# Where a preparation step is done: layer 2's weights and the image norms of samples 1 to 3, in a four-layer network on one NeuronCore

## The chip, the core and the metric

The kernel runs on one core of one Trainium2 chip. A core has five engines that run side by side, each working through its own instructions in order: TensorE (PE in the profile; its weight loads are PEld), VectorE (DVE), ScalarE (ACT), GpSimd (POOL) and SyncE (SP), which here issues nearly all transfers between the core's memory and DRAM. An instruction that depends on another engine or on a transfer waits for a semaphore, and all that stands behind it on its engine waits with it. The metric is the device time of one execution in microseconds (us); lower is better.

## The reference, cut to what matters

The input x is float32, (4, 56, 56, 128): four samples, 56 x 56 positions, 128 channels. Four layers follow, each a residual around a group norm:

```python
x = x + L0(gn(x))    # 7x7 window attention, then attention over all 3136 positions, then an MLP
x = x + L1(gn(x))    # for each node: sum over 56 partners of relu(a_i + b_j), then a linear layer
x = x + L2(gn(x))    # Fourier layers: keys, queries, values, attention over 128 channels, projection, ...
x = x + L3(gn(x))    # a convolution over one axis with its row and column sums
```

Layer 2 treats each of the 128 channels of a sample as a 56 x 56 image. What the change touches is its beginning:

```python
xa = x.reshape(B * T, 1, H, W)                     # T = 128 images in each of B = 4 samples
xa_n = _inorm(xa, norm_g[0], norm_b[0])            # (x - mean) * rsqrt(var + eps) over an image
k = _fno_layer(xa_n, wK, wKs, bKs, (H // 2, W // 2))   # rfft2, times weights per frequency, irfft2
q = _fno_layer(xa_n, wQ, wQs, bQs, (H // 2, W // 2))
v = _fno_layer(xa_n, wV, wVs, bVs, (H, W))
scores = jnp.einsum('bhtd,bhsd->bhts', qs, ks) / np.sqrt(ks.shape[-1])
```

The kernel works with the images' spectra. Scores come from spectra and from products of the key and query weights; values and projection are merged into one set of weights for each frequency. Both sets depend on the weights alone, not on x.

## The kernel before, in words

**Layers 0 and 1** run one sample after another (`first_layers`). Each sample has four stages: the 7x7 tiles (`fast_windows`, eight groups in a software pipeline whose order on PE, ACT and DVE is written out by hand), attention over all positions (lines 606 to 684), the MLP (lines 856 to 940) and the edge layer (lines 982 to 1050), which leaves the sample in the tile `x1`. One SP transfer then saves `x1` to DRAM (`x2d[b]`, line 2484), and another loads the next sample (`xw`, line 2477).

**Image norms.** `normed_images` is a Python generator: it issues a norm in small steps, each `yield` ending one. Its steps are 56 `bn_stats` over the rows of the images (line 1243, two to a step), one `bn_aggr` (1247), two small PE products with `k.g4` that average over groups of four channels (1250, 1259), about twenty short DVE operations on 128 x 56 or 128 x 1, two square roots on ACT (1274, 1301), two PE products over the 128 partitions' sums (1283, 1292), and four passes over the image that subtract the mean and scale (line 193 by way of `apply_norm`), after which SP stores the normed sample to `xad[b]` (1299). It keeps an inverse deviation for each image in `st.norm`. Before the change the norms of samples 0, 1 and 2 are dealt out between the stages of `fast_windows` of samples 1, 2 and 3 (`steps = beside(bank)`, one step after each pipeline stage).

**Spectra.** After the last edge layer, `spectra` transforms the four samples. `first_transform` of a sample makes four `s_pr` tiles (PE, 56 matmuls each in the profile, line 1322), scales each on DVE with the image's inverse deviation into `s_z` (1324) and copies it on ACT (1326). `sample_spectra` of a sample then issues thirteen steps: three `s_ps` (PE 1338, ACT copies 1341), two `s_pr2` (PE 1350, ACT 1354) and eight `s_px` (PE 1360, evacuated by DVE and ACT in turn, line 232 or 230). The four pieces of the next sample's `first_transform` are issued at steps 2, 5, 7 and 9, and the norm of sample 3, the only one left, at three of its steps after each step. PE, ACT and DVE keep the order in which all this is written. Samples 0 to 2 come from `xad` into two tiles `s_x2` (line 2516, two transfers of 784 KB each); sample 3 is still in `x1`.

**Layer 2's weights.** `all_score_weights` loads `qk4`, `qk` and `qkr` and combines them on GpSimd into `g` and `g4`; `value_weights` loads `V`, `Vrev` and `P`, combines them on GpSimd and stores the result to DRAM (`dd`). Both are issued just ahead of `spectra`, in the pool `g_wk`. `attention_weights`, which follows the spectra, is the first to read `g`.

**Queues around the change.** SP's transfers go out in program order. Where the program is not ordered by hand (SP, and GpSimd here), a scheduler sets the order. Behind the branch that joins the samples' loop, SP's order before is: the four loads of `s_x2` for samples 0 and 1, then `qk4` and `qk`, the store of `x1` to `x2d[3]`, eight small weights, `qkr`, `V`, `Vrev`, `P`, and the two loads for sample 2.

## Time and profile before

| | us |
|---|---|
| median of 6 runs | 3877.62 |
| lowest and highest of them | 3871.62, 3890.88 |
| the profiled execution, device time | 3868.63 |
| the profiled execution, span of its instructions | 3866.6 |
| 7x7 tiles of sample 0, first `w_xg` to first `f_s` | 98.86 |
| the same of samples 1, 2, 3 | 111.68, 111.77, 111.78 |
| spectra, first `s_pr` to first `q_u` on DVE | 2884.43 to 2971.58 |

Over the whole span PE is busy 91%, DVE 75%, ACT 54% and GpSimd 31%. The shares are averages over stages with different limits, so the stage that an edit lies in has to be looked at by itself. PEclk is the clock that TensorE was granted, as a share of full speed. A line of the timeline gives the start, the duration, the engine, the source line, the operation, the tile written and the tiles read, the shape, and how many equal instructions were merged; in brackets stands the idle time ahead of it and what ended that.

### The profile page before, as it was taken

How to read it: one execution, taken by the hardware profiler on the slowest of the kernel's cores; microseconds unless marked ns; L12 is line 12 of the kernel's file. 1: busy time of each engine (PE TensorE's matmuls, PEld its weight loads, DVE VectorE, ACT ScalarE, POOL GpSimd, SP SyncE). 2: the span in 40 equal slices, each digit the busy share in tenths (PEclk: the TensorE clock that was granted, in tenths of full speed). 3: DMA queues.
4: the chain of work that ended last, by engine and by line, in shares of the span. 5: the costliest groups of instructions: out<-in, count | busy, mean ns of one | idle time of the engine just before them, and what ended most of it. 6: DMA issues, size and time to landing. Idle time of an engine off the chain costs nothing. (4 is left out here: it accounts for less than half of the span.)

```text
span 3866.6 us, 79430 instructions
## 1 busy us (share of the span) xinstructions
PE 3537.0 (91%) x35416; PEld 1584.9 (41%) x35416; DVE 2896.0 (75%) x2703; ACT 2077.9 (54%) x2080; POOL 1210.9 (31%) x667
## 2 busy tenths in 40 slices
PE   6899999989998998999989989999998979989988
PEld 4322234543223455323245532223456433336564
DVE  6588877858887786788869758887776767765654
ACT  4577765548776554677745457776542012214332
POOL 0000016600000570000028300000655769975556
PEclk8999999999999999999999999999998999999888
DMA  2000000000000000000000000000011058841101
GB/s 96 1 1 1 1 1 19 19 17 1 1 1 1 18 3 34 1 1 1 1 17 3 19 18 1 1 1 34 2 42 51 1 119 171 171 107 59 52 8 50
DMA packets 73496, 111.12 MB, mean 29 GB/s; under 512 B 62140, under 2 KB 63932, under 8 KB 67900
## 3 DMA queue, kind: packets, MB, share of 16 engines
q1 hardware_dynamic: 14460, 93.13, 8.1%
q10 hardware_dynamic: 58688, 12.85, 2.0%
q8 instruction: 279, 4.57, 0.5%
q14 instruction: 69, 0.57, 0.1%
HBM read 79.46 MB, written 26.51 MB: 27 GB/s over the span
## 5 line engine op out<-in xcount | busy, mean ns | idle before, releaser
L663 ACT ACTIVATE f_ring<-f_s 128x1792 f32<-128x1792 f32 (+3 forms) x796 | 1097.3, 1429 | 226.6 <-PE f_s L661 224.8
L606 DVE TENSOR_TENSOR f_acc<-f_acc,f_ring 128x1792 f32<-128x1792 f32 x560 | 1133.9, 2025 | 64.3 <-ACT f_ring L663 7.5
L661 PE MATMUL f_s<-f_qT,f_kT 32*128 32x448 f32 x5376 | 738.4, 571 | 47.9 <-ACT f_ring L663 29.5
L877 POOL TENSOR_TENSOR m_sq<-m_y 128x392 f32<-128x392 f32 x16 | 14.5, 919 | 1973.8 <-ACT m_y L876 1973.7
L612 PE MATMUL f_po<-f_ring,f_va 128*32 128x448 f32 x5376 | 589.7, 546 | 0.0
L1029 DVE TENSOR_TENSOR e_td<-e_pa,e_c 128x1792 f32<-128x1792 f32 x252 | 491.2, 2012 | 14.4 <-ACT e_a L994 14.4
L1031 POOL TENSOR_TENSOR e_tp<-e_a,e_c 128x1792 f32<-128x1792 f32 x140 | 451.8, 3258 | 145.2 <-PE e_acc L1036 104.4
L661 PEld LDWEIGHTS f_s<-f_qT,f_kT 32*128 32x128 f32 x5376 | 268.3, 183 | 524.6 <-ACT f_ring L663 379.1
L1036 PE MATMUL e_acc<-e_td,t_shared 32*32 32x448 f32 x8064 | 324.0, 546 | 22.0 <-DVE e_td L1029 11.2
L1033 ACT ACTIVATE e_tp<-e_tp 128x1792 f32<-128x1792 f32 x140 | 235.1, 1697 | 176.4 <-POOL e_tp L1031 176.4
L1645 DVE TENSOR_TENSOR u_ud<-u_px,u_d 112x1792 f32<-112x1792 f32 x144 | 240.1, 1707 | 94.8 <-PE u_po L1650 85.7
L612 PEld LDWEIGHTS f_po<-f_ring,f_va 128*32 128x32 f32 x5376 | 133.0, 109 | 396.5 <-issue 395.5
L1036 PE MATMUL e_acc<-e_tp,t_shared 32*32 32x448 f32 x4480 | 222.4, 547 | 3.2 <-ACT e_tp L1033 2.5
L1650 PE MATMUL u_po<-u_ud,AT 112*64 112x448 f32 x960 | 200.7, 548 | 23.3 <-DVE u_ud L1645 23.3
L1647 POOL TENSOR_TENSOR u_up<-xh,u_d 112x1792 f32<-112x1792 f32 x64 | 193.8, 3056 | 24.0 <-PE u_po L1650 12.4
L1036 PEld LDWEIGHTS e_acc<-e_td,t_shared 32*32 32x32 f32 x8064 | 134.3, 103 | 146.3 <-DVE e_td L1029 55.9
L629 DVE RECIPROCAL f_den<-f_den 128x448 f32<-128x448 f32 x28 | 82.7, 2953 | 77.3 <-ACT f_den L628 77.3
L1650 PE MATMUL u_po<-u_up,AT 112*64 112x448 f32 x576 | 125.2, 541 | 0.8 <-POOL u_up L1647 0.8
L1650 PEld LDWEIGHTS u_po<-u_ud,AT 112*64 112x64 f32 x960 | 64.9, 137 | 147.6 <-issue 86.7
L606 DVE TENSOR_TENSOR f_acc<-f_ring 128x1792 f32<-128x1792 f32 x28 | 56.7, 2024 | 86.7 <-ACT f_ring L663 57.8
L1512 POOL TENSOR_TENSOR q_u<-iS,q_g 128x1792 f32<-128x1792 f32 x32 | 102.7, 3236 | 56.7 <-PE s_px L1360 32.5
L1036 PEld LDWEIGHTS e_acc<-e_tp,t_shared 32*32 32x32 f32 x4480 | 95.2, 103 | 55.4 <-ACT e_tp L1033 19.4
(485 smaller groups left out, 4785.0 us busy)
## 6 DMA issues: line engine op xcount, KB each, us to landing
u_d<-dd SPq DMA_DIRECT2D x48, 784.0 KB
xw<-in_x SPq DMA_DIRECT2D x4, 1568.0 KB
x2d<-x SPq DMA_DIRECT2D x4, 1568.0 KB
xad<-x SPq DMA_DIRECT2D x4, 1568.0 KB
x_xs<-xad ACTq DMA_DIRECT2D x32, 196.0 KB
xm<-x_ev ACTq DMA_DIRECT2D x64, 98.0 KB
o_a<-xm SPq DMA_DIRECT2D x8, 784.0 KB
o_x<-x2d SPq DMA_DIRECT2D x4, 1568.0 KB
```

The costliest lines, as they stand in the source:

```text
L606: nc.vector.tensor_add(acc, slots(j, 0) if c == 1 else acc, slots(j, c))
L612: nc.tensor.matmul(po[heads[h], :NB], va[o, c, heads[h]], p, start=(c == 0), stop=(c == 24))
L661: nc.tensor.matmul(ss[:, i, :NB], kT[heads[h], c * P:(c + 1) * P], qT[heads[h], blk(j)], start=True, stop=True)
L663: nc.scalar.activation(ring[:, slot:slot + m, :], ss[:, :m, :NB], AF.Exp, scale=scale)
L1029: nc.vector.tensor_tensor(t, am, cm, ALU.max)
L1031: nc.gpsimd.tensor_sub(t, bc(a.rearrange("p (l n) -> p l n", l=8), 1, 4), cm)
L1033: nc.scalar.activation(tf, tf, AF.Relu)
L1036: nc.tensor.matmul(acc[quarters[q], r, :NB], k.ident[o, o], t[o, q].rearrange("p l n -> p (l n)"), start=(g == 0), stop=(g == len(EDGE_TUR ...
L1512: nc.gpsimd.tensor_mul(u, bc(st.iS[:, bp, c, :HH], 1, HEADS), bc(g[:, n, c, :], 2, HH))
L1645: nc.vector.tensor_mul(u, bc(px[:, :, :NB], 2, m), dm)
L1647: nc.gpsimd.tensor_mul(u, bc(x, 2, m), dm)
L1650: nc.tensor.matmul(po[64 * b2:64 * b2 + 64, :NB], st.AT[:, 8 * i + h0 + q, 2 * bp + b2, :], u[:, b2, q, :], start=(left == 16), stop=(left ...
```

## The change

Three things are edited.

1. Layer 2's weights are made in sample 0's pass: `norms(0, ...)` calls `layer2_weights()` and returns an empty iterator. The score weights go to DRAM as one tile `gd` of 17 columns and are loaded back into `g` ahead of the spectra. `value_weights` no longer copies into a third tile; it stores from `d` and from `V`.
2. Of the norms, only sample 0's stays beside 7x7 tiles (those of sample 1). The tiles of samples 2 and 3 carry none. Samples 1 and 2 are read for the spectra from `x2d`, not yet normed.
3. In `spectra` the order of samples becomes 0, 3, 1, 2. The norms of 3, 1 and 2 are dealt out one after another, three steps after each piece of sample 0's first transform and four after each step of `sample_spectra`. The next sample's first transform is issued at steps 8 to 11; ahead of its first piece, the steps of that sample's norm that are left are issued.

```diff
@@ spectra
-        norm = normed_images(k, w, st, B - 1, wk, lambda: tiny.tile([P, 512], F32, name="s_pt"), st.x1, xad[B - 1])
+        order = [0, B - 1, *range(1, B - 1)]
+        def of(b):
+            return st.x1 if b == B - 1 else images(b)
+        def steps(n):
+            for norm in norms[:1]:
+                for _ in range(n):
+                    if next(norm, norm) is norm:
+                        norms.pop(0)
+                        break
+        norms = [normed_images(k, w, st, b, wk, lambda: tiny.tile([P, 512], F32, name="s_pt"), of(b), xad[b])
+                 for b in order[1:]]
         zs = {}
-        first = [first_transform(k, st, b, (wk, psum), st.x1 if b == B - 1 else images(b), zs) for b in range(B)]
+        first = [first_transform(k, st, b, (wk, psum), of(b), zs) for b in order]
         for _ in first[0]:
-            pass
-        for b in range(B):
+            steps(3)
+        for i, b in enumerate(order):
             for n, _ in enumerate(sample_spectra(k, st, b, (wk, psum), zs.pop(b))):
-                for _ in range(3):
-                    next(norm, None)
-                if b < B - 1 and n in (2, 5, 7, 9):
-                    next(first[b + 1])
+                if i < B - 1 and 8 <= n < 12:
+                    while n == 8 and len(norms) + i >= B - 1:
+                        steps(1)
+                    next(first[i + 1])
+                steps(4)
@@ value_weights
-    f = wk.tile([P, 3, 8, HH], F32, name="d_f")
...
-    nc.gpsimd.tensor_copy(f[:, 0], d[:, 0])
-    nc.gpsimd.tensor_sub(f[:, 1], d[:, 1], d[:, 0])
-    nc.gpsimd.tensor_add(f[:, 2], d[:, 0], d[:, 1])
-    nc.sync.dma_start(dd.rearrange("n g h i x -> (g h i) n x"), f.rearrange("p n c r -> p n (c r)"))
+    nc.gpsimd.tensor_sub(w.V[:, 0], d[:, 1], d[:, 0])
+    nc.gpsimd.tensor_add(w.V[:, 1], d[:, 0], d[:, 1])
+    to = dd.rearrange("n g h i x -> (g h i) n x")
+    nc.sync.dma_start(to[:, 0:1], d[:, 0:1].rearrange("p n c r -> p n (c r)"))
+    nc.sync.dma_start(to[:, 1:3], w.V.rearrange("p n c r -> p n (c r)"))
@@ all_score_weights
-    st.g = pool.tile([P, 2, 16, HEADS], F32, name="q_g")
-    st.g4 = pool.tile([P, 2, 1, HEADS], F32, name="q_g4")
+    g = wk.tile([P, 2, 17, HEADS], F32, name="q_g")
...
+    nc.sync.dma_start(gd, g)
@@ build
+            def layer2_weights():
+                with tc.tile_pool(name="g_wk", bufs=1, side="right") as wk:
+                    all_score_weights(k, I, w2, wk, gd)
+                with tc.tile_pool(name="d_wk", bufs=1, side="right") as wk:
+                    value_weights(k, I, w2, wk, dd)
             def norms(b, bank):
-                if b < 0:
+                if b == 0:
+                    layer2_weights()
+                if b != 1:
                     return iter(())
-                return normed_images(k, w2, st, b, io, bank, x1w, xad[b])
+                return normed_images(k, w2, st, 0, io, bank, x1w, xad[0])
...
-                    first_layers(lambda *a: fast_attention(*a, functools.partial(norms, b - 1), k.mr[:, b, :]), I["x"][b],
+                    first_layers(lambda *a: fast_attention(*a, functools.partial(norms, b), k.mr[:, b, :]), I["x"][b],
...
-                    nc.sync.dma_start(xp[:, t:t + 28, :], xad[b, :, t:t + 28, :])
+                    nc.sync.dma_start(xp[:, t:t + 28, :], (x2d if b else xad)[b, :, t:t + 28, :])
...
-                with tc.tile_pool(name="g_wk", bufs=1, side="right") as wk:
-                    all_score_weights(k, I, w2, sp, wk, st)
-                    value_weights(k, I, w2, wk, dd)
-                    spectra(k, w2, st, xad, images)
+                g = sp.tile([P, 2, 17, HEADS], F32, name="g")
+                nc.sync.dma_start(g, gd)
+                st.g, st.g4 = g[:, :, :16], g[:, :, 16:]
+                spectra(k, w2, st, xad, images)
```

The second branch of the program, for inputs whose scores are not small, is changed likewise and does not run here.

## The prediction

> **What bounds the kernel now.** I read the stages that the edits touch, first the 7x7 tiles of the four samples: busy time of each engine from the first `w_xg` to the first `f_s` of each.

> ```profile
> core 0: us, PE busy (x) PEld busy (x) DVE busy (x) ACT busy (x) POOL busy (x), PEclk, DMA share, GB/s
> 50.62:149.48 98.86, 88.59 (x714) 53.98 (x715) 52.88 (x99) 47.05 (x79) 8.69 (x22) 0.94 0.00 1
> 749.15:860.83 111.68, 94.87 (x732) 57.31 (x732) 68.53 (x183) 48.14 (x82) 8.75 (x22) 0.92 0.07 30
> 1458.92:1570.69 111.77, 94.86 (x732) 57.28 (x732) 68.51 (x183) 48.12 (x82) 8.74 (x22) 0.92 0.07 30
> 2172.29:2284.07 111.78, 94.86 (x732) 57.26 (x732) 68.53 (x183) 48.14 (x82) 8.75 (x22) 0.92 0.07 30
> ```

> Sample 0 carries no norm and takes 98.9 us; the others carry one (84 more DVE instructions) and take 111.8. A norm costs 12.9 us there: PE works by a fixed order and waits for the norm's short chain. Next the spectra, cut where their character changes.

> ```profile
> 2884.00:2905.00 21.00, 19.26 (x444) 17.36 (x444) 12.31 (x65) 8.33 (x18) 8.67 (x24) 1.00 0.80 270
> 2905.00:2929.00 24.00, 13.16 (x96) 10.96 (x95) 20.58 (x44) 2.90 (x8) 23.90 (x32) 0.58 0.02 5
> 2929.00:2972.00 43.00, 41.35 (x672) 36.24 (x670) 16.23 (x25) 21.70 (x48) 5.27 (x5) 1.00 0.19 67
> ```

> At both ends PE is the limit. In the middle it is idle for half the time: there DVE works off sample 3's norm, with GpSimd's weights beside it. The order of PE's instructions shows what that does to its clock.

> ```profile
> 2908.61 0.38 PE L1250 MATMUL s_pt<-s_mv,t_shared 128*128 128x1 f32 x2 [3.43 <-DVE s_mv L1247]
> 2908.93 3.20 PE L1322 MATMUL s_pr<-t_images,s_x 128*64 128x33 f32 x56
> 2933.18 1.83 PE L1322 MATMUL s_pr<-t_images,s_x 128*64 128x33 f32 x56
> ```

> ```profile
> SPq L2516 <- DVE f_oT L630: 411.6, 1, 411.6
> SPq L158 <- PE e_po L1004: 212.5, 1, 212.5
> ```

> ```profile
> 2669.01 1.91 SPq L2516 DMA_DIRECT2D s_x<-xad  x4
> 2883.58 0.81 SPq L158 DMA_DIRECT2D t_w_qk<-in_w_qk  x2
> ```

> Samples 0 and 1 are loaded at 2669, during sample 3's MLP, 215 us ahead of their use. The weights come behind, since their memory is free only when the last edge matmul has ended.

> **The change part by part.** *Tiles of samples 2 and 3.* Each loses a norm and should look like sample 0: 2 x 12.9 = 25.8 us off. The stores to `xad` leave with it; SP waited for DVE there, and nothing behind it was urgent. Bounds: 20, if PE's half clock falls otherwise, and 28.

> *Tiles of sample 0.* GpSimd gets its weights here: it was busy 8.67 + 23.90 us with them up to 2929, some 36 us in all, less the 0.9 us copy. After its memsets (done at 59.6) it has nothing to do before the MLP at 550. SP issues seven loads and three stores; behind them its queue holds `xw`, which was issued at 591. Both queues hide this. The cost can only come by way of DVE: at 50.62 a `w_xg` operation beside a memset took 1.79 us against a median of 0.48. Six more of them fall beside the weights, and two groups of lead cover them. Below: 0; above: 6 x 1.3 = 8. I take 1.5, near the lower end since PE did not wait for these.

> *Loads of samples 0 and 1.* In the changed program's order SP's first transfer behind the join is `g<-gd`, ahead of the loads of `s_x`. Its semaphore counts are those of the stage's end: PE count 14,472, where `t_w_qk` waits for 14,480 in the program before, less the 2 x 4 products of the two norms that left the tiles. So it goes at 2883.6, and the images, free to go at 2669, queue behind it. The transfers between 2673 and 2678 ran at 408 to 439 GB/s. 0.56 MB of `g` and 0.80 MB of half an image take 3.2 us, after some 2 us until they run: PE's first `s_pr` starts near 2889.1 instead of 2884.4. This costs 4.7 us (bounds 3.5 and 7). DVE's order has the first `s_z` ahead of all norm steps, so the norm of sample 3, which needs no load, is late by as much.

> *Spectra at full clock.* DVE's rows for one norm:

> ```profile
> 2891.75 2.21 DVE L1243 BATCH_NORM_STATS2 s_rows<-x 128x6 f32<-128x56 f32 x18
> 2906.90 1.66 DVE L1247 BATCH_NORM_AGGREGATE s_mv<-s_rows 128x2 f32<-128x336 f32 x1
> ```

> A `bn_stats` takes 0.123 us, 56 of them 6.9. In the changed order, three pieces of the next transform alternate with `s_px` from the first `s_z` of a sample to its last: 3 x (1.75 + 0.83) = 7.75 (24 `bn_stats` fit between). Then one path runs through DVE and PE: `s_z` 0.6, 32 `bn_stats` 3.95, aggregate 1.66, two products with three DVE operations 1.2, `s_pr2` with its copies and the root behind them on ACT 1.9, three DVE operations 0.7, product 0.68, copy and difference 0.4, an `s_px` and its DVE copy 1.45, two operations 0.45, product 0.68, copy 0.15, and three `s_px` and an `s_pr` 4.25, which cover the four scalings (0.62 each without GpSimd). Sum 25.8 us for a sample, where PE alone needs 16.6 (`s_ps` at 2944.41 and at 2960.98). Along the stage: 2889.1; four `s_pr` and an `s_z` 7.6; 38 `bn_stats` 4.7; the chain of sample 3, 25.8 - 7.75 - 0.6 - 3.95 = 13.5, less 0.75 (`s_pr2` is done by then) and 1 (one `s_px` instead of three ahead of the `s_pr`), with 3 for the twenty `conv_weights` operations in it, 14.7; so its first `s_z` is at 2916.1. Two samples later it is 2967.7. The last sample needs 18.3 of PE's work: 2986.0, against 2970.2 before. At full clock the stage grows by 16 us; this holds the 4.7 of the loads and the gain of some 7 us from GpSimd leaving (DVE operations of 0.2 us took 1.1 beside it between 2909 and 2928).

> *Spectra at half clock.* PE will be idle for 5.7 us ahead of the first `s_pr`, and for about 3.6 us in each sample before the first product; 3.43 us sufficed above. The first four `s_pr` then take 4 x 1.4 = 5.8 more. From the products to the next `s_z`, half clock adds 0.75 (`s_pr2`), 0.85 and 2.5 (`s_px`) and 1.45 (`s_pr`), 5.5 for a norm. Nearest rows: the dip at 2909 lasted until 2929, that at 2974, under dense products, only 3.4 us. I take 4 of the 5.5: 5.8 + 3 x 4 = 18. Below: 0. Above: half clock through the alternation as well, 3 x (1.45 + 0.86) = 6.9 more for each of three samples, 43 in all.

> [...]

> *What is hidden.* Three stores to `xad` now run inside the spectra, on a queue where only `apart` and `q_Tp` follow; the last goes out some 15 us ahead of them and needs 4. Without that cover `q_u` would start up to 4 us later. Sample 2's load waits for sample 0's transforms as before, over 30 us ahead of its norm.

> Sum: -25.8 + 1.5 + 16 + 18 = +9.7, say +10. The profiled execution (3868.63; the span is 2 us less) becomes 3878.6. It lies 9 us below the median of the runs, 3877.6; moved by the same, that becomes 3888.

> **The rivals.** *The clock holds.* Where the dips cost under 10 us, nothing is lost. At 0 the sum is -8.3, 3869; with the loads in time as well -13, 3865. For it: the idle times of 3.6 us are barely longer than those that sufficed, and the 1.0 us ahead of `s_pr` at 2884 cost no clock. Against: two idle times of 3.3 and 3.4 us were enough, and the 5.7 us at the start are safe. *Half clock throughout.* PE then takes 26 us for a sample's transforms and sets the pace instead of DVE: +10 + 25 = 3912 at the end, 3903 if one sample of three recovers. For it: the row at 2908.93; against: `s_ps` brought the clock back at 2929. *The weights disturb sample 0's tiles.* All 8 us are paid: 3894. For it the 1.79 us row; against it, most DVE operations there read PSUM, and those were not longer beside GpSimd in the spectra (`s_z` 0.62 to 0.64). *Nothing is gained in the tiles,* because something else waits: the three equal rows of 111.7 to 111.8 against 98.9 leave no room for it.

> **How the numbers follow.** Forecast, 3888 with a range of its own of 3879 to 3896: 0.42. The clock holds, 3860 to 3878: 0.30. Half clock throughout: 0.20. Disturbed tiles: 0.08. A difference under 0.2% (7.8 us, hence 3869.8 to 3885.4) can't be told from none. Of the forecast 0.17 lies inside that band and 0.25 above; of the first rival 0.20 below and 0.10 inside; the others above. So faster 0.20, same 0.27, slower 0.53. The range leaves out a tenth on each side: 3866 to 3906.

> **What would show it.** The tiles of samples 2 and 3 at 99 us, sample 0's at 99 to 102. SP's `s_x` loads at the edge layer's end behind `g`, the first `s_pr` some 5 us after `e_po`. First `s_z` of successive samples 26 to 31 us apart instead of 16.6, with PE waiting for `s_mv`. From the first `s_pr` to `q_u` some 115 us (counted from 2884 in the old time: 121) instead of 87. The prediction is wrong if `s_x` goes out ahead of `g`, or if PEclk stays at 1.00 through the spectra.

## The result, and the profile after

The changed kernel takes 3885.90 us (median of 30 runs, 3874.72 to 3897.37), the kernel before 3875.83 beside it (67 runs, 3864.58 to 3895.37): a ratio of 1.0024, with a 95% interval of 1.0018 to 1.0031. It is slower by 0.24%, some 9 to 10 us. The profiled executions say the same: spans of 3875.9 and 3866.6 us, 9.3 apart.

First the stages of the changed kernel, by the busy time of each engine in stretches. The columns are those of the prediction's tables: the stretch and its length, then PE, PEld, DVE, ACT and POOL with their instructions, the granted clock, DMA. Rows one to four are the 7x7 tiles of samples 0 to 3, then sample 3's attention over all positions, then the spectra from the last `e_po` to the first `q_u`.

```profile
50.70:148.94 98.24, 88.58 (x714) 54.34 (x715) 53.96 (x99) 46.97 (x79) 42.21 (x73) 0.94 0.10 36
...
748.76:860.49 111.73, 94.90 (x732) 57.29 (x732) 68.51 (x183) 48.15 (x82) 8.74 (x22) 0.92 0.07 30
...
1458.62:1557.94 99.32, 88.43 (x724) 54.92 (x724) 53.83 (x102) 47.70 (x80) 8.77 (x22) 0.97 0.04 17
...
2159.71:2258.20 98.49, 86.71 (x724) 54.77 (x724) 53.80 (x102) 47.71 (x80) 8.77 (x22) 0.98 0.04 18
2258.20:2643.99 385.79, 363.91 (x3036) 110.99 (x3036) 324.85 (x167) 292.75 (x223) 0.00 (x0) 0.99 0.00 1
...
2861.21:2977.60 116.39, 85.83 (x1224) 74.70 (x1224) 66.27 (x295) 33.76 (x76) 2.30 (x8) 0.81 0.30 110
```

The weights lie in sample 0's row (POOL is busy 42.21 us there instead of 8.69), and the row takes 98.24 us against 98.86. (Before and after, sample 0's row ends 1.9 us ahead of its first `f_s`, at 149.48 instead of 151.35 before; the other samples' rows end 0.1 us ahead of theirs.) Samples 2 and 3 have lost their norms and 25.7 us. The spectra took 88.15 us before (2883.43 to 2971.58) and take 116.39 now.

With the stretches behind the tiles counted in, the difference of the spans is made up like this:

| stretch | before | after | difference |
|---|---|---|---|
| sample 0, all of it | 698.5 | 698.1 | -0.5 |
| sample 1 | 709.8 | 709.9 | +0.1 |
| sample 2 | 713.4 | 701.1 | -12.3 |
| sample 3 | 711.1 | 701.5 | -9.6 |
| spectra | 88.2 | 116.4 | +28.2 |
| behind them, to the end | 895.0 | 898.3 | +3.3 |

Sample 3 keeps 9.6 of its 13.3: its attention takes 385.79 instead of 382.86, all of it PE's busy time (363.91 instead of 360.98), and the stretch behind it 0.7 more. The granted clock is at half in this attention from 2263.5 to 2270.4 and for its last 1.6 us; before it was for its last 0.3 alone, and for 17.1 us in the tiles ahead of it, where 3.4 are left now. Part of the half clock has moved from the tiles into the stretch behind them.

Now the spectra, cut where sample 0's transforms end, first before, then after.

```profile
2883.43:2892.00 8.57, 6.84 (x226) 6.76 (x226) 3.41 (x8) 1.87 (x4) 2.73 (x11) 1.00 0.86 313
2892.00:2971.58 79.58, 66.93 (x984) 57.80 (x984) 45.75 (x127) 30.68 (x69) 34.98 (x48) 0.87 0.23 75
```

```profile
2861.21:2879.70 18.49, 9.74 (x225) 9.54 (x225) 5.44 (x25) 1.76 (x4) 1.27 (x7) 0.72 0.87 308
2879.70:2977.60 97.90, 76.09 (x1000) 65.16 (x1000) 60.83 (x272) 32.01 (x73) 1.03 (x1) 0.83 0.19 73
```

The start costs 10 us more, the rest 18.3. SP's timeline of the changed kernel (start, us, line, transfer) and PE's (start, us, line, matmul, and in brackets the idle time before it and what ended it) show why.

```profile
2861.34 0.33 SPq L2562 DMA_DIRECT2D g<-gd  x1
2861.86 2.00 SPq L2541 DMA_DIRECT2D s_x<-xad  x2
2863.90 0.91 SPq L2541 DMA_DIRECT2D s_x<-x2d  x2
```

```profile
2868.35 7.21 PE L1322 MATMUL s_pr<-t_images,s_x 128*64 128x33 f32 x145 [7.15 <-DMA s_x<-xad]
...
2911.73 0.38 PE L1250 MATMUL s_pt<-s_mv,t_shared 128*128 128x1 f32 x2 [3.59 <-DVE s_mv L1247]
...
2936.55 1.84 PE L1338 MATMUL s_ps<-s_z,t_images 128*128 128x56 f32 x6
...
2966.98 1.84 PE L1338 MATMUL s_ps<-s_z,t_images 128*128 128x56 f32 x6
```

`g` is first and the images go at the join, so PE waits 7.15 us (1.0 before), and most of the 145 `s_pr` behind the wait run at half clock, which ends at 2874.5. Later PE waits for every norm's aggregate, 3.29 us for the first and 3.59 for the other two, and a sample takes 30.4 us (2936.55 to 2966.98) where PE alone needs 16.6 (the last period before). PE's waits in this stage, in total, times and longest:

```profile
PE s_pt L1250 <- DVE s_mv L1247: 10.5, 3, 3.6
PE s_pr L1322 <- DMA s_x<-xad: 7.1, 1, 7.1
PE s_pt L1283 <- DVE s_mean L1279: 4.7, 3, 1.9
```

### The profile page after: what moved, and what is told of

Read it like the earlier page. It is cut to its first block, busy times and chain, and to the rows that moved or that the text cites. A ratio compares the mean times of both kernels' runs of the same rounds, so it can differ in the third digit from the quotient of the medians.

```text
span 3875.9 us, 79439 instructions
## 1 busy us (share of the span) xinstructions
PE 3544.8 (91%) x35416; PEld 1593.3 (41%) x35416; DVE 2884.6 (74%) x2703; ACT 2078.5 (54%) x2080; POOL 1208.8 (31%) x666
## 5 line engine op out<-in xcount | busy, mean ns | idle before, releaser
L1029 DVE TENSOR_TENSOR e_td<-e_pa,e_c 128x1792 f32<-128x1792 f32 x252 | 491.2, 2012 | 14.4 <-ACT e_a L994 14.4
L1664 POOL TENSOR_TENSOR u_up<-xh,u_d 112x1792 f32<-112x1792 f32 x64 | 193.8, 3053 | 25.8 <-PE u_po L1667 12.4
L1529 POOL TENSOR_TENSOR q_u<-iS,g 128x1792 f32<-128x1792 f32 x32 | 102.7, 3235 | 120.5 <-PE s_px L1360 97.3
```

Source lines behind the costliest of these rows:

```text
L1029: nc.vector.tensor_tensor(t, am, cm, ALU.max)
L1664: nc.gpsimd.tensor_mul(u, bc(x, 2, m), dm)
```

## The experiments

All twelve are in this table. Times count from the last `e_po`; a period is the distance of one sample's first `s_ps` from the next one's; half clock is the time that PEclk stood at 0.50 between the last `e_po` and the first `q_u`. Ratios are to the kernel before, run beside each. One run of each kernel was traced: the columns up to half clock are from it, the median and the ratio from all runs. In e1, e6 and e12 the traced run took 3901.7, 3893.5 and 3883.1 us, 5 to 9 above the median, so their long periods and half clock need not be what most of their runs did.

| kernel | first s_ps | periods | q_u | half clock | median us | ratio, 95% interval |
|---|---|---|---|---|---|---|
| before | 8.5 | 31.2, 21.3, 16.6 | 88.1 | 20.5 | 3875.8 | |
| after | 18.5 | 26.6, 30.2, 30.4 | 116.4 | 44.4 | 3885.9 | 1.0024, 1.0018 to 1.0031 |
| e1 g on ACT | 21.5 | 35.9, 28.3, 30.3 | 126.7 | 78.5 | 3892.4 | 1.0037, 1.0022 to 1.0051 |
| e2 weights only | 14.9 | 26.4, 19.5, 16.6 | 87.9 | 17.1 | 3879.3 | 1.0004, 0.9989 to 1.0020 |
| e3 norms only | 14.4 | 47.5, 29.4, 30.3 | 132.3 | 81.9 | 3896.3 | 1.0049, 1.0033 to 1.0066 |
| e4 filler | 17.8 | 30.8, 30.2, 30.2 | 119.7 | 10.2 | 3882.4 | 1.0018, 1.0004 to 1.0033 |
| e5 short filler | 17.4 | 28.9, 25.8, 25.9 | 108.6 | 13.7 | 3871.9 | 0.9985, 0.9972 to 0.9998 |
| e6 early images | 16.3 | 36.9, 28.4, 30.4 | 122.6 | 68.3 | 3884.2 | 1.0012, 0.9996 to 1.0028 |
| e7 weights, early images | 8.5 | 23.1, 17.9, 16.6 | 76.7 | 3.4 | 3865.4 | 0.9965, 0.9952 to 0.9978 |
| e8 paced | 17.0 | 21.7, 21.2, 20.4 | 90.8 | 17.1 | 3851.6 | 0.9927, 0.9910 to 0.9944 |
| e9 paced, late stores | 14.0 | 22.8, 21.2, 20.4 | 89.0 | 13.7 | 3845.3 | 0.9920, 0.9905 to 0.9934 |
| e10 late stores | 14.6 | 38.0, 28.4, 30.4 | 122.0 | 71.7 | 3884.4 | 1.0022, 1.0011 to 1.0033 |
| e11 e9, code shifted | 10.8 | 24.5, 21.2, 20.4 | 87.5 | 10.2 | 3851.4 | 0.9935, 0.9916 to 0.9954 |
| e12 e10, code shifted | 8.5 | 38.0, 28.3, 30.2 | 115.5 | 58.0 | 3878.5 | 1.0005, 0.9995 to 1.0016 |

### e1: the images ahead of g

```diff
-                nc.sync.dma_start(g, gd)
+                nc.scalar.dma_start(g, gd)
```

> The changed kernel with one edit: g is loaded by ACT's queue, so SP issues the four image loads first; these wait only for GpSimd's last e_tp of the edge layer (ended 2851.58 in the changed kernel), 10 us before the layer's end. Theory (the loads queued behind g are part of the loss): first s_pr within 1.5 us of the last e_po instead of 7.2, the first 145 s_pr without their half clock, the stage from the last e_po to q_u 107 to 110.5 us instead of 116.4, time 6 to 9 us under the changed kernel: 3877 to 3880, ratio to the kernel before 1.0003 to 1.0011. Rival (sample 3's norm sets the pace, its statistics would fill DVE while PE waits, so that the loads are hidden): the stage stays at 115 to 117, ratio 1.0024.

A miss: 1.0037, no better than the change itself (1.0024; the intervals overlap). The images went at 2858.25, 9.6 us ahead of the end of the last `e_po` at 2867.8, and still the first `s_pr` came 3.98 us behind it. PE's timeline:

```profile
2871.79 1.14 PE L1322 MATMUL s_pr<-t_images,s_x 128*64 128x33 f32 x17 [3.98 <-DMA s_x<-x2d]
2877.26 11.31 PE L1322 MATMUL s_pr<-t_images,s_x 128*64 128x33 f32 x207 [4.33 <-issue]
```

Seventeen `s_pr`, then 4.33 us in which PE waits for nothing that the profile names, then everything at half clock, where it stood for all but 3.4 of the 58 us from 2870.8 to 2928.9. To move a load out of a wait was not enough; something else stood behind it.

### e2: the weights alone

The changed `layer2_weights` at sample 0, `g` by ACT's queue, and the norms and spectra of before (of its edits, the one to the norms beside the tiles):

```diff
             def norms(b, bank):
                 if b == 0:
                     layer2_weights()
-                if b != 1:
+                if b == 0:
                     return iter(())
-                return normed_images(k, w2, st, 0, io, bank, x1w, xad[0])
+                return normed_images(k, w2, st, b - 1, io, bank, x1w, xad[b - 1])
```

> Only the first half of the change: layer 2's weights beside sample 0's tiles (g by ACT's queue), norms where the kernel before has them. Theory (GpSimd beside DVE in the spectra cost some 7 us, in the tiles nothing): tiles of samples 1 to 3 at 111.7, sample 0's at 98 to 99, from the last e_po to q_u 79 to 83 us instead of 88.2, the idle time of PE between 2905 and 2929 shorter, time 5 to 9 us under before: ratio 0.9977 to 0.9987. Rival (the norm's chain through PE and the half clock fill that stretch anyway): 87 to 89 us, ratio 0.9995 to 1.0005. Rival 2 (the weights disturb the tiles on most runs): sample 0 over 100, ratio above 1.

The time did not move (1.0004), as the rival had it, but for another reason: from the first `s_ps` to `q_u` it is 73.0 us instead of 79.6, the 6.6 us that the theory gave to GpSimd's leaving, and the first `s_ps` comes 6.4 us later. The images went late here too, at 2877.3, 9.7 us ahead of the end of the last `e_po`, but PE did not wait for them: it stood for 3.00 us ahead of its first `s_pr` and for 3.14 us after 113 of them, both with no wait that the profile names. In e7, which differs only in where the branch that doesn't run makes its weights, and so in the time of these loads, the second stop is gone and the first `s_pr` comes after 1.04 us.

### e3: the norms alone

Norms and spectra as in the changed kernel, the weights made by GpSimd in the spectra as before, their loads by ACT's queue (of its edits, one of these loads):

```diff
-    load_weights(k, wk, I, "w2_", w, ("qk", "qkr", "qk4"))
+    load_weights(k, wk, I, "w2_", w, ("qk", "qkr", "qk4"), queue=nc.scalar)
```

> Only the second half: norms of samples 1 to 3 in steps inside the spectra, GpSimd's weights made there as before (their loads by ACT's queue so that the images go first). Theory (GpSimd slows DVE's small operations, and the half clock comes with them): tiles of samples 2 and 3 at 98 to 99.5, but the stage from the last e_po to q_u at 116 to 122 us: 110 without the load delay and 6 to 12 for the contention, which falls into the first two norms (some 36 us of GpSimd). Ratio 1.002 to 1.004. Rival (contention costs nothing where PE and the clock set the pace): 107 to 111 us, as with g on ACT, ratio 1.0003 to 1.0011.

The direction is the theory's, the size is beyond it: `q_u` comes at 132.3, the first period is 47.5. DVE's timeline beside GpSimd:

```profile
2880.59 0.64 DVE L1255 TENSOR_TENSOR s_t<-s_mv,s_mr 128x1 f32<-128x1 f32 x1
2881.27 7.73 DVE L1256 SCALAR_TENSOR_TENSOR s_t<-s_t,s_mv 128x1 f32<-128x1 f32 x1
```

The second operation takes 0.22 us in the changed kernel. Here GpSimd started twelve operations while it lasted, and PE waited 8.69 us for it instead of 0.70. Not all of e3's loss is GpSimd's: PE also stopped for 2.01 us at the start, and its clock stood at half for most of the first period. The kernel to compare it with is e10 below, which has such a stop and half clock too, but no GpSimd work: its first period is 38.0 and its `q_u` at 122.0, so GpSimd beside the norms costs some 10 us here. That is why the two halves of the change belong together.

### e4 and e5: PE's idle time filled

```diff
+        def fill(ps, n):
+            for _ in range(n):
+                nc.tensor.matmul(ps[:, 256:512].rearrange("p (v m) -> p v m", v=2), k.fs[:, 0, :], k.fs[:, 0:2, :],
+                                 start=True, stop=True)
...
     ps = bank()
+    if fill:
+        fill(ps, 13)
     nc.tensor.matmul(ps[:, 0:1], k.g4, mv[:, 0:1], start=True, stop=True)
```

and the same with 2, 9 and 4 ahead of a norm's other products; in e5 with 7, 1, 4 and 2.

> The changed kernel with idle time of PE in the norms filled: 13, 2, 9 and 4 matmuls of 128x256 ahead of a norm's four products, some 0.24 us each, into unused columns of the same bank, read by nobody. The start (7 us without PE) is left as it is. Theory (half clock is 10 to 14 us of the stage): PEclk 1.00 from the second sample on, s_px at 0.5 us for 4 instead of 0.9, distance of successive first s_z 30.2 down to 26 to 28, time 5 to 12 us under the changed kernel: ratio 0.9993 to 1.0011. Rival (DVE's chain sets the pace, PE's slow matmuls lie in its shadow, or the fillers stand in the products' way): 30 us a sample still, ratio 1.002 to 1.004.

> The changed kernel with fillers of the right length. In the run with 13, 2, 9 and 4 fillers each took 0.43 us instead of the 0.24 assumed, the first group 5.8 us, and the products came 2.0, 0.4, 2.0 and 0.5 us after DVE had their operands, 4.9 a sample, with the distance of samples unchanged at 30.2 and no half clock. Now 7, 1, 4 and 2 of them (3.0, 0.4, 1.7 and 0.9 us). Theory (a sample takes 25.8 at full clock and the half clock costs 4 to 5): 25 to 26.5 us from one sample's s_ps to the next, half clock only at the stage's start, time 9 to 14 us under the changed kernel: ratio 0.9988 to 1.0003. Rival (DVE's chain sets 30 us at any clock): 29 to 31 us, ratio 1.0018 to 1.003.

e4 does not tell the two theories apart: a filler took 0.43 us where 0.24 was assumed, and the products came late by about what the clock had saved. With e5's lengths the answer is plain. First e5, then the changed kernel's two lines above: the distance is 25.87 us instead of 30.43.

```profile
2933.19 1.84 PE L1346 MATMUL s_ps<-s_z,t_images 128*128 128x56 f32 x6
...
2959.06 1.84 PE L1346 MATMUL s_ps<-s_z,t_images 128*128 128x56 f32 x6
```

Matmuls whose result nobody reads are all that e5 adds to the changed kernel, and they took it from 1.0024 to 0.9985: 13.7 us of half clock are left of 44.4, all in the first 24 us. At full clock DVE's chain sets 25.8; half clock adds 4.4 and 4.6 to the last two periods. The first period, 28.9, did not come down to the 25 to 26.5 that were expected.

### e6 and e7: the images loaded early again

In the branch for general scores the weights are made ahead of the loop. That takes GpSimd's last `e_tp` out of what the images' memory waits for, and they go at 2652 in e6. `g` goes by ACT.

```diff
             with small.Else():
+                layer2_weights()
                 with tc.For_i(0, B, 1) as b:
...
-                layer2_weights()
```

> The changed kernel with the images of samples 0 and 1 loaded at about 2645 again, during sample 3's MLP: the weights of the other branch (general scores) are made ahead of its loop, so that the images' memory no longer waits for GpSimd's last e_tp, and g goes by ACT's queue. In the run with g on ACT alone the images still went at 2858, in the edge layer's last 10 us, and PE stood for 4.0 and 4.3 us more with no wait that the profile names, while 16 KB pieces of the instruction queue came 1.7 us and, after 17 matmuls, 6 us later. Theory (transfers at the join, of images or in front of PE's code, are the loss): first s_pr 1 to 2 us after the last e_po, first s_ps at 8.5 to 10 us instead of 18.5, q_u 105 to 109 us after the last e_po instead of 116.4; ratio 0.9997 to 1.0008. Rival (PE's code comes late whatever is loaded, since g and x2d still go out at the join): first s_ps at 13 us or more, ratio 1.0012 or more.

> Weights beside sample 0's tiles, norms as before, images loaded early again. With the images late, the stretch from sample 0's s_ps to q_u was 73.0 us against 79.6 before, 6.6 us off, and the first s_ps came 6.4 us later: together nothing. Theory: both are separate, so this kernel keeps the first and loses the second: first s_ps at 8.5 to 9.5, q_u 80 to 83 us after the last e_po, time 5 to 8 us under before: ratio 0.9979 to 0.9988. Rival (the norm of sample 3 ends the same time after the join, so that a wait moves and nothing is won): q_u at 86 to 89, ratio 0.9996 to 1.0006.

In e7 (norms of before) it did what was expected, and more: first `s_ps` at 8.5, `q_u` at 76.7, half clock for 3.4 us, and 0.9965. In e6 (norms of the change) the first `s_pr` came after 1.0 us, but PE stood still for 1.50 us after 17 of them and 3.94 us after 128 more, the clock fell, and of the 10 us only 2.2 were won at the first `s_ps`. e6 fits its rival, that PE's instructions come late; what shows it stands in the last section.

### e8: another pace of the norms

On top of e6:

```diff
+        steps(8)
         for _ in first[0]:
-            steps(3)
+            steps(5)
...
                     next(first[i + 1])
-                steps(4)
+                steps(1 if i == n == 0 else (0, 0, 2, 5, 2, 2, 1, 2, 8, 8, 8, 5, 0)[n])
```

> The changed kernel with early images and another pace of the norms: 48 of a sample's 56 bn_stats within the alternation and the rest and the aggregate behind its last s_z (16 stats there in place of 8), the products behind s_ps, s_pr2 and single s_px. DVE then has 2.6 us of work beside 2.7 of PE in each turn of the alternation. Theory (the chain behind the last s_z sets the pace: 32 bn_stats, 3.95 us, leave it, and the idle time of PE and with it the half clock shrink): 20 to 24 us a sample, q_u 82 to 95 us after the last e_po, ratio 0.9925 to 0.996. Rival (DVE becomes the bound in the alternation, or the small products stall PE as often as before): 26 to 30 us, ratio 0.998 to 1.0008.

Right on all counts: periods of 21.7, 21.2 and 20.4, ratio 0.9927.

```profile
2904.95 1.90 PE L1338 MATMUL s_ps<-s_z,t_images 128*128 128x56 f32 x6 [0.63 <-DVE s_z L1324]
2907.61 0.38 PE L1250 MATMUL s_pt<-s_mv,t_shared 128*128 128x1 f32 x2 [0.76 <-DVE s_mv L1247]
...
2926.12 1.90 PE L1338 MATMUL s_ps<-s_z,t_images 128*128 128x56 f32 x6 [0.64 <-DVE s_z L1324]
```

PE waits 0.76 us for the aggregate instead of 3.59, and after the start the clock doesn't fall again before `q_u`. The norm's work is the same; 24 `bn_stats` of a sample have moved from behind its last `s_z` to between the first ones (32 stood behind it, 8 do now), and the steps after the aggregate are dealt out between smaller pieces of PE's work.

### e9 and e10: stores behind the first transforms

The store of `x2d` and the load of `g` go out by ACT, behind its copies of sample 0's `s_z`; e9 stands on e8, e10 on e6.

```diff
+                def later():
+                    nc.scalar.dma_start(x2d[B - 1], x1)
+                    nc.scalar.dma_start(g, gd)
...
         for _ in first[0]:
             steps(5)
+        later()
```

> The paced kernel with the store of x2d (1.57 MB) and the load of g (0.56 MB) issued by ACT behind its copies of sample 0's s_z, some 8 us after the join, instead of at it; only the small weights of the last layers still go out at the join. In the paced run PE did 17 s_pr, then stood 3.28 us with no wait named while a 16 KB piece of its queue took 2.26 us among the data (0.88 to 1.2 us elsewhere), and the half clock that followed doubled the next 207: first s_ps at 17.0 us after the last e_po where 8.5 is possible (before, and weights with early images). Theory (the pieces of code wait behind the data, and the idle time costs the clock): first s_ps at 8.5 to 11, half clock at the start gone, q_u 82 to 86 us after the last e_po instead of 90.8, ratio 0.9900 to 0.9915. Rival (entering this stretch costs PE its 3 us whatever the queues move): first s_ps at 14 or more, ratio 0.992 to 0.9935.

> The changed kernel's own order of norms, images loaded early, x2d and g behind sample 0's s_z: what the join's transfers cost in the change, all of them taken away. Theory (as for the paced kernel): first s_ps at 8.5 to 11 us instead of 18.5 (changed kernel) and 16.3 (images early alone), the samples behind it at 27 to 31 us as in the changed kernel, q_u 104 to 110 us after the last e_po instead of 116.4; ratio 0.9995 to 1.0010. Rival (PE's stop belongs to the join): first s_ps at 14 or more, ratio 1.001 or more.

The theory misses the point of both, and the rivals hold. e9 has the lowest median of all (0.9920, an interval that overlaps those of e8 and e11), but its first `s_ps` is at 14.0, and e10's at 14.6: PE stops after 17 `s_pr` with little on the queues (in e10 25, 186 and 12 GB/s in the three microseconds from 2864 on, where e6's first stop had 273 to 303). e10's timeline:

```profile
2864.20 0.68 PE L1322 MATMUL s_pr<-t_images,s_x 128*64 128x33 f32 x17 [1.00 <-DVE x L1009]
2866.95 10.13 PE L1322 MATMUL s_pr<-t_images,s_x 128*64 128x33 f32 x207 [2.07 <-issue]
```

The 207 behind the stop run mostly at half clock. With data at the join the stops are longer in sum (3.28 us in e8, 2.00 in e9; 1.50 and 3.94 in e6, 2.07 in e10), but the one after 17 `s_pr` comes without them.

### e11 and e12: code that never runs

```diff
+                    pad = psum.tile([P, 512], F32, name="n_ps")
+                    for _ in range(16):
+                        nc.tensor.matmul(pad[:, 0:1], k.g4, k.g4[:, 0:1], start=True, stop=True)
                     xp = xs.tile([P, HH, HH], F32, name="n_x")
```

These lines stand in the branch for general scores, which these inputs don't take; e11 is e9 with them, e12 is e10.

> The paced kernel with late stores, and one edit that never runs: 16 matmuls of one column in the branch for general scores, 64 more PE instructions in the program ahead of the join. Everywhere the changed order of norms was used, PE stopped after exactly 17 s_pr (or did 17 and then 128), also with no data on the queues (2.0 us); with the norms of before it does 224 without a stop. Pieces of PE's queue are 16 KB, and 128 s_pr with their weight loads fit one if an instruction has 64 bytes. The norms taken from the tiles leave 62 to 64 fewer PE instructions ahead of the join. Theory (the join's first piece ends after 17 s_pr by its position in the program): no stop in the first 100 s_pr, first s_ps at 8.5 to 9.5 us instead of 14.0, half clock at the start gone, q_u 82 to 85 us after the last e_po instead of 89.0; ratio 0.9900 to 0.9912. Rival (the stop belongs to something else in the changed order): 17 s_pr and a stop of 2 us as before, first s_ps at 14, ratio 0.992.

> The same 64 instructions that never run, in the kernel with the changed kernel's own order of norms, early images and late stores: now nothing of the join's cost should be left in it, and what the norms' steps cost in the spectra stands alone. Theory: first s_ps at 8.5 to 9.5 us instead of 14.6 (and 18.5 in the changed kernel), the sample behind it at 26 to 31 us, not 38, since the first 224 s_pr keep the clock; q_u 104 to 108 us after the last e_po; ratio 0.9995 to 1.0008. Rival (the half clock comes from the first norm's wait all the same and holds through the first alternation): first s_ps at 8.5 to 9.5 but 34 to 38 us behind it, ratio 1.001 to 1.002.

The stop is gone in both. e12's timeline:

```profile
2865.07 6.72 PE L1322 MATMUL s_pr<-t_images,s_x 128*64 128x33 f32 x224 [1.00 <-DVE x L1009]
```

All 224 `s_pr` run through, and the first `s_ps` is at 8.5, as before the change. In e12 that is worth 5.9 us by the medians (3884.4 to 3878.5) and 6.5 at `q_u`. Its first period, however, is 38.0, as the rival had it: behind the first norm's wait of 3.30 us the clock is at half. So against the changed kernel the traced run has won 10 us at the first `s_ps` and only 0.9 at `q_u`. The traced run took 3883.1 us at a granted clock of 0.955 over the whole span; seven of the twelve runs took 3873.7 to 3878.7 at 0.958. Whether they too had the long period is open. In e11 the first `s_ps` comes at 10.8, since DVE stops there for 2.28 us with no wait named and the first `s_z` are late; `q_u` is 1.5 us earlier than in e9, not the 4 to 7 that were expected. The whole is not faster than e9: the stretch from `q_u` to the end took 898.5 us in e11's profile and 890.1 in e9's, though no edit lies there. Some of that is clock (141 us at half instead of 130). The rest is open, and so is which of the two is faster.

## Why the prediction was right

It named 3888 us, slower, +10 on the span; measured were 3885.9 and +9.3. The direction and the paths were right; that the total came out so close is partly luck, as its terms show one by one:

- *Tiles of samples 2 and 3, -25.8.* The tiles gave 25.7 (99.32 and 98.49 instead of 111.8). The size was luck: the 12.9 us of a norm came from sample 0's row, which ends 1.9 us ahead of its first `f_s`. To its first `f_s` sample 0 took 100.7 us, 11 less than the others, which would have made 22 for two. That 3.6 of it would come back as half clock behind sample 3's tiles was not foreseen; the whole is -21.9, inside the bounds of 20 to 28.
- *Sample 0 beside the weights, +1.5.* It is -0.6. The rival of disturbed tiles falls: DVE was busy for 53.96 us instead of 52.88, and PE did not wait for it.
- *Loads, 4.7.* PE waits 7.15 us instead of 1.0, 6.1 more and within the bounds: `g` first, as forecast, then `s_x`. That the images could go at 2669 otherwise was wrong: their memory also waited for GpSimd's last `e_tp` (they went at 2858 in e1), and PE made stops behind them in which it waited for nothing that the profile names (4.33 us in e1, 1.50 and 3.94 in e6).
- *Spectra at full clock, 25.8 us for a sample.* The step that e5 tests directly: 25.8 and 25.9 in its last two periods. And e2 tests the gain from GpSimd's leaving, put at 7: 6.6, or 11.5 in e7, where PE does not stop at the start.
- *Half clock, 18.* Mis-sized, in the changed kernel's profile. The start gave 18.5 - 8.5 - 6.1 = 3.9 instead of 5.8 (which should have been 4 x 1.4 = 5.6), and 0.9 of the 3.9 is PE's stop after 145 `s_pr`. The last two periods gave 4.4 and 4.6 where 4 was taken. For the first period no run shows any: it took 26.6, and 28.9 in e5. That makes some 12. It is no fixed price: e12, with the norms in the same order, stood at half for 58.0 us in this stage, e10 for 71.7.
- *The sum.* The spectra grew by 28.2 instead of 34. The 6 too much, and 2 too much for sample 0, are offset by the 3.6 behind the tiles and 3.3 us behind the spectra, for which the prediction had nothing and no experiment here a cause; behind the spectra the clock stood at half for 151.5 us instead of 138.5. The total is better than its terms.
- *Its signs.* The tiles without a norm, the place of `g` and `s_x`, PE's waits for `s_mv` and the distance of the samples came as named. The first `s_pr` came 7.15 us behind the last `e_po` instead of some 5, and from it to `q_u` it was 109 us instead of 115.

In e12 busy time of PE alone did not bring the full clock back. The prediction's row at 2908.93 is 3.20 us of `s_pr` at half clock; a longer stretch of e12, by the columns of the first table:

```profile
2891.05:2910.51 19.46, 19.46 (x258) 18.61 (x257) 9.31 (x43) 3.61 (x7) 0.00 (x0) 0.50 0.20 85
```

PE is busy for all 19.46 us, and the clock stays at 0.50.

Of the rivals, the one in which the clock holds is what e5 built, but for the start: it was put at 3869, and e5 took 3871.9. Half clock throughout (3903 to 3912) was not reached by any kernel; e1 and e3, with some 80 us of it, came to 3892 and 3896.

So the change is three things: weights out of the spectra, a gain of 6.6 us (e2) or 11.5 with the images early (e7: `q_u` at 76.65 instead of 88.15); two norms from the tiles into the spectra, -21.9 there and 18.3 + 6.6 = +24.9 here; and 10 us at the join, without which both e7 and e12 start. The three don't simply add: in e12's trace the first period took the 10 us back.

## What to carry to other kernels

A step that is moved into a gap costs what its chain adds there, not what its instructions take: count what stands behind the last operation that it must follow, and move work ahead of that point (with the images early in both, e8 went from e6's 1.0012 to 0.9927 by the order of the same instructions). What a change does to the order of transfers at a join has a price of its own (here PE waited 7.15 us instead of 1.0), so look at the first transfer in the queue and at what its memory waits for. When PE stops without a named wait right behind a branch (2.07 us in e10), look at the records of its instruction queue as well as at its data.

## What the hardware showed that was not expected

*Code position.* In every kernel with the changed norms and images that came in time, PE did 17 `s_pr` behind the join (19 in e3) and stopped (2.01 us in e3, 1.50 in e6, 3.28 in e8, 2.00 in e9, 2.07 in e10); 16 matmuls that never run took the stop away in e11 and e12. The instruction queue's records (q8) are 16 KB pieces, 279 of them with 4.57 MB on the page of the kernel before. Over PE's 35,416 matmuls and 35,416 weight loads there, that is 64.5 bytes for each; that they are PE's is an estimate from this. They took 0.9 to 1.4 us each in most places and 2.26 in e8, between the transfers of `x2d` and `g`. In all these stops PE went on 1.36 to 1.46 us after such a piece had ended (in e10 the piece ended at 2865.49, PE went on at 2866.95), and so it did in e1 (1.26), after 113 `s_pr` in e2 (1.36), after 145 in the changed kernel (1.58: the piece ended at 2874.86, PE went on at 2876.44) and, before the change, at a stop of 0.58 us in the spectra (1.45: 2893.44 and 2894.89). That speaks for these pieces as what it waited for. e6's second stop came 128 `s_pr` behind the first, and the changed kernel's after 145, which is 17 and 128. That the pieces' borders set the 17 is what this, e11 and e12 support; the borders themselves are not in the trace.

*DVE beside GpSimd.* The operation of 7.73 us in e3 reads columns of one element in each partition (128x1). Twelve GpSimd operations of 0.24 to 1.39 us started while it lasted. In the changed kernel, where GpSimd runs nothing from 2879.3 to 2976.5, the same operation took 0.22 us, at 2886.90 and at 2912.54. How the one slows the other, no run here isolates.

*The clock's way back.* It came back to full under `s_ps` in e12 at 2913.6 after 34 us, and under `s_pr` alone in the changed kernel at 2874.5, 6.2 us after the first of them. `s_pr` alone at half clock for longer didn't bring it back in e8 (most of 11.31 us) and in e9 (some 7.4 us of 9.61, an estimate from the granted clock of 0.71 between 2863.70 and 2877.76). What decides it is open.
